# Turned one-hots from ScalarE out of the penalties, and seven tiles of a block weighed on VectorE, in a graph attention layer

## The chip, the core and the metric

The kernel runs on one core of one Trainium2 chip. The core has five engines with queues of their own: TensorE (PE; PEld for its weight loads), VectorE (DVE), ScalarE (ACT), GpSimd (POOL) and SyncE (SP). Each takes its instructions in the order in which they were written; between engines only semaphores keep order. The metric is device time in microseconds. A profile shows one execution.

## What is computed

Two graph layers with residual and layer norm on 20,000 nodes of 256 features, with 340,000 edges that are sorted by destination: a relational layer (two rounds of messages with a weight matrix for each of 8 edge types), then graph attention with four heads of 64 features. The change touches the attention alone:

```python
h = (x @ W).reshape(n, NHEAD, OUT_F)
hl = jnp.sum(a_l * h, axis=-1)
hr = jnp.sum(a_r * h, axis=-1)
e = jax.nn.leaky_relu(hl[row] + hr[col], negative_slope=ALPHA)
e_max = jax.ops.segment_max(e, row, num_segments=n)
...
ee = jnp.exp(e - e_max[row])
denom = jax.ops.segment_sum(ee, row, num_segments=n)
att = ee / denom[row]
msg = att[:, :, None] * h[col]
out_h = jax.ops.segment_sum(msg, row, num_segments=n)
...
x = _layernorm(x + _L1_gnn_ref(x, edge_index, L1_gnn_W, L1_gnn_a_l, L1_gnn_a_r), axis=-1)
```

For every node `row` the edges that start there compete: the greatest score is taken off, the exponentials are the weights, and the weighted rows `h[col]` are added up and divided by the sum of the weights.

## The kernel before

Nodes come in 157 blocks of 128, one node to a partition. The edges of a block are laid into 17 tiles of 128 edges (`T3 = 17`), one edge to a partition. Before the attention two rounds compute the relational layer, sort the edges by their other end and write a row of 270 float32 (1080 bytes) for each node into `table3s`: the 256 features of `h`, four `hr`, four `hl`, and `hr` once more in three bfloat16 parts.

The attention is `attention` with its function `step(i)`, called for i = 0 to 157 under an order written out by hand (`manual_schedule`): nothing is moved by a scheduler. Three blocks are in work in a step: a (block i), b (i - 1) and c (i - 2). Tiles carry the letters of the profile:

- `load(b)`, L1360: 17 gathers on POOL, each of which brings the `table3s` rows of a tile's 128 edges into `g`; L1358, a plain load on SP, brings the block's own rows as an eighteenth tile. Four buffers of `g` turn, so the gathers of block i + 2 wait until the last `sums` of block c = i - 2 is done.
- `load_ob`, L1344: five loads on SP, which spread the ids of each edge's own node over all partitions (`ob`, bfloat16, 128 x 17 x 128).
- `ends(a, 0..2)`, L1404 and L1406: TensorE turns the three parts of `hr` onto 12 rows, ScalarE copies them out (`hpt`). Parts are six, six and five tiles.
- `distances(a, 0..2)`, L1382: on ScalarE, `pen = (FAR * (ob - row))^2` with FAR = 2^50: 0 where the edge belongs to the node of this partition, at least 2^100 where not.
- `greatest(a, part, head)`, L1417 and L1420: TensorE spreads one head's `hr` of six tiles over all partitions (`pr`, two buffers), and VectorE takes `pr - pen` and its maximum along the row in one instruction. There are twelve in a step, 3 parts x 4 heads; the text calls them compares, one to twelve.
- `one_hots(a)`, L1388: on VectorE, `s[edge, node]` = 1 where the edge is the node's. It is the matrix by which `sums` adds up.
- `turned_hots(a)`, L1394: on VectorE, the same one-hots the other way round, `st[node, edge] = (ob == row)` in bfloat16, 128 x 2176 elements. In the next step `spread(b)`, L1440, multiplies by it to bring each node's terms to its edges.
- `own_terms(b)`, L1428 to L1431 and, through `split`, L1300 and L1303: small VectorE instructions on the maxima of block b. They open a step.
- `weights(b)`, L1445 to L1453: VectorE forms the scores, ScalarE the exponentials, once into PSUM (`pw`) and once into `g`. 
- `weigh_few(b, tiles)`, L1468: VectorE multiplies the 256 features of several tiles by their weights, in one instruction. `weigh(b, tiles)`, L1462: ScalarE does the same with four instructions of 128 x 64 for each tile, one a head.
- `sums(b, tiles)`, L1476: TensorE multiplies the one-hots by the weighted rows, in float32, and accumulates a block's 18 tiles in `po`.
- `finish`, `measure`, `write` (L1482 to L1513): quotient, residual, layer norm; `write` works on four blocks at a time, with a square root on ScalarE, so that every fourth step loads another function table and the step after it loads that of the exponential again.

The second half of `step` is a loop n = 1 to 9. Each turn has one `sums(b, [n])`, the weighing on ScalarE of a tile some turns ahead, and one or two further compares; `turned_hots` stands behind the compare of turn 5, `distances` of parts 1 and 2 in turns 1 and 3, `write` in turn 4. TensorE thus alternates between a compare's two matmuls, which wait for VectorE to have freed a `pr` buffer, and the two passes of a float32 `sums`, which wait for the weighing.

A last block with fewer than 8 tiles takes the branch `few`, once in the whole run.

Of the kernel before, what the change touches and what calls it, by code (L numbers as in the profile page):

```python
# [35 lines left out]
BF16 = mybir.dt.bfloat16  # L36
# [3 lines left out]
AF = mybir.ActivationFunctionType  # L40
ALU = mybir.AluOpType
# [6 lines left out]
P = 128  # L48
# [9 lines left out]
T3 = 17  # L58
# [16 lines left out]
def gnn_kernel(  # L75
# [17 lines left out]
    nc = tc.nc  # L93
# [83 lines left out]
    ones = const.tile([P, P], F32, name="ones")  # L177
# [8 lines left out]
    row_of = const.tile([P, 1], F32, name="row_of")  # L186
# [1120 lines left out]
    def attention(words):  # L1307
        with tc.tile_pool(name="ac", bufs=1) as cp, tc.tile_pool(name="ag", bufs=4) as gp, \
# [20 lines left out]
            parts = [(q, min(6, T3 - q)) for q in range(0, T3, 6)]  # L1329
# [35 lines left out]
            def others(k):  # L1365

                n = k["n"]
                k["ob"] = obs.pop(k["b"])
                k["pen"] = sp.tile([P, T3, P], BF16, name="pen")
                k["hpt"] = turns[k["b"] % 2]  # L1370

                k["top"] = sp.tile([P, H, 1 + len(parts)], F32, name="top")
                nc.scalar.copy(k["top"][:, :, 0], k["g"][:, n, D:SR])
                k["hl"] = sp.tile([P, 2, H], F32, name="hl")
                nc.scalar.copy(k["hl"][:, 0, :], k["g"][:, n, SR:SR + H])  # L1375

            def distances(k, i):

                q, m = parts[i]
                m = min(m, k["n"] - q)  # L1380
                if m > 0:
                    nc.scalar.activation(k["pen"][:, q:q + m], k["ob"][:, q:q + m], AF.Square, bias=away, scale=FAR)  # L1382

            def one_hots(k):

                s = k["s"] = sp.tile([P, T3, P], F32, name="s", bufs=3)
                n = k["n"]
                nc.vector.tensor_tensor(s[:, :n], pi.unsqueeze(1).to_broadcast([P, n, P]),  # L1388
                                        own3[:, k["b"], :n].unsqueeze(2).to_broadcast([P, n, P]), op=ALU.is_equal)

            def turned_hots(k):

                k["st"] = sp.tile([P, T3, P], BF16, name="st")
                nc.vector.tensor_scalar(k["st"][:, :k["n"]], k["ob"][:, :k["n"]], row_of, None, op0=ALU.is_equal)  # L1394

            def ends(k, i):

                q, m = parts[i]
                m = min(m, k["n"] - q)
                if m <= 0:  # L1400
                    return
                ph = p2.tile([P, 6, P], F32, name="pr")
                for t in range(q, q + m):
                    nc.tensor.matmul(ph[:3 * H, t - q, :], k["g"][:, t, SR + H:].bitcast(BF16), identb,  # L1404
                                     start=True, stop=True)
                nc.scalar.copy(k["hpt"][:3 * H, q:q + m, :], ph[:3 * H, :m, :])  # L1406
# [19 lines left out]
            def own_terms(k):  # L1426
                z = sp.tile([P, H], F32, name="z")
                nc.vector.tensor_reduce(z, k["top"][:, :, :1 + -(-k["n"] // 6)], op=ALU.max, axis=AX.X)  # L1428
                hl = k["hl"]
                nc.vector.tensor_add(z, z, hl[:, 0, :])  # L1430
                nc.vector.scalar_tensor_tensor(hl[:, 1, :], z, SLOPE, z, op0=ALU.mult, op1=ALU.max)  # L1431
                k["hlp"] = split(sp, hl.rearrange("p a h -> p (a h)"), [2 * H], "hlp")

            def spread(k):

                k["pe"] = p1.tile([P, 512], F32, name="pe")
                n = k["n"]
                pe = k["pe"][:, :(n + 1) * 6 * H].rearrange("p (t c) -> p t c", t=n + 1)
                for t in range(n + 1):
                    nc.tensor.matmul(pe[:, t], k["st"][:, t, :] if t < n else identb, k["hlp"], start=True, stop=True)  # L1440
# [14 lines left out]
            def weigh(k, ts):  # L1455

                for t in ts:
                    if t > k["n"]:
                        return
                    gh = k["g"][:, t, :D].rearrange("p (h f) -> p h f", h=H)  # L1460
                    for h in range(H):
                        nc.scalar.activation(gh[:, h, :], gh[:, h, :], AF.Copy, scale=k["g"][:, t, D + h:D + h + 1])  # L1462

            def weigh_few(k, ts):

                t, n = ts[0], len(ts)
                gh = k["g"][:, t:t + n, :D].rearrange("p t (h f) -> p t h f", h=H)
                nc.vector.tensor_mul(gh, gh, k["pw"][:, t:t + n, :].unsqueeze(3).to_broadcast([P, n, H, HF]))  # L1468

            def sums(k, ts):  # L1470
                n = k["n"]
                for t in ts:
                    if t == 0:
                        k["po"] = p2.tile([P, SR], F32, name="po")
                    if t <= n:
                        nc.tensor.matmul(k["po"], k["s"][:, t, :] if t < n else ident, k["g"][:, t, :SR],  # L1476
                                         start=(t == 0), stop=(t == n))
# [39 lines left out]
            def step(i):  # L1517

                a, b, c = (blocks.get(x) for x in (i, i - 1, i - 2))
                if b:
                    own_terms(b)
                if a:
                    others(a)
                    ends(a, 0)
                    distances(a, 0)
                if c:
                    sums(c, [11, 12])
                    weigh(c, [16])  # L1530
                if b:
                    spread(b)
                if a:
                    one_hots(a)
                if c:
                    sums(c, [13])
                if a:
                    ends(a, 1)
                if c:
                    weigh(c, [17])  # L1540
                    sums(c, [14])
                if a:
                    ends(a, 2)
                if c:
                    sums(c, [15, 16])
                if b:
                    load_x(b)
                if b and not a:

                    weights(b)  # L1550
                    for t in range(0, b["n"] + 1, 6):
                        weigh_few(b, list(range(t, min(t + 6, b["n"] + 1))))
                        sums(b, range(t, min(t + 6, b["n"] + 1)))
                    if c:
                        sums(c, [17])
                        finish(c)
                        measure(c)
                        write(c)
                    finish(b)
                    measure(b)  # L1560
                    write(b)
                    return
                if b:
                    weights(b)
                    weigh_few(b, [0, 1])
                    weigh_few(b, [2, 3, 4])
                if a:
                    greatest(a, 0, 0)
                if c:
                    sums(c, [17])  # L1570
                    if c["b"] + 4 < NB:
                        blocks[c["b"] + 4] = load(c["b"] + 4)
                load_ob(i + 2, 0)
                if a:
                    greatest(a, 0, 1)
                if b:
                    sums(b, [0])
                if a:
                    greatest(a, 0, 2)
                if c:  # L1580
                    finish(c)
                few = a and a["n"] < 8
                for n in range(1, 10):
                    if a and n in (1, 3):
                        distances(a, (n + 1) // 2)
                    if b:
                        sums(b, [n])
                        if few and n in (1, 4, 7):
                            weigh_few(b, [n + 5, n + 6])
                        if not few or n in (1, 4, 7):  # L1590
                            weigh(b, [n + 4])
                        if n == 9:
                            weigh(b, [14, 15])
                    if a:
                        greatest(a, (n + 2) // 4, (n + 2) % 4)
                        if n == 5:
                            turned_hots(a)
                    if n in (2, 4, 6, 8):
                        load_ob(i + 2, n // 2)
                    if c and n == 1:  # L1600
                        measure(c)
                    if c and n == 4:
                        write(c)
                if b:
                    sums(b, [10])
# [330 lines left out]
```

## Time and profile before

Five runs took 13794.76 to 13819.41 us, with a median of 13805.79 us.

| | |
|---|---|
| profiled execution, its own time | 13803.91 us |
| its span | 13801.8 us |
| mean granted TensorE clock | 0.852 |
| PE busy | 9911.7 us (72%) |
| PEld busy | 7524.2 us (55%) |
| DVE busy | 7552.4 us (55%) |
| ACT busy | 5946.9 us (43%) |
| POOL busy | 7624.3 us (55%) |

"Busy" sums the durations that an engine's instructions have in the record. A line of a group gives the line of code, the engine, the operation, what it writes from what, the count, then busy time and the mean of one in nanoseconds, then the engine's idle time just before them and what ended it. The largest groups of the attention, over the whole run:

```profile
L1360 POOL DMA_INDIRECT g<-table3s,words x2657 | 2540.3, 956 | 2826.5 <-PE po L1476 1999.6
L1420 DVE CUSTOM_DVE_ANT_0 dump<-pr,pen 128x768 bf16<-128x768 f32 x1876 | 1654.6, 910 | 1981.7 <-remote 1321.2
L1462 ACT ACTIVATE g<-g 128x64 f32<-128x64 f32 x8088 | 2065.1, 334 | 438.3 <-issue 437.9
L1476 PE MATMUL po<-g,s 128*128 128x260 f32 x5314 | 2025.1, 480 | 85.2 <-DVE g L1468 85.2
```

Instructions of an engine overlap at their ends, so the starts of two `weigh` instructions can lie closer together than the 334 ns that one lasts.

### The profile page before, as it was taken

The page shows a single profiled execution, that of the slowest core. Times are in us where ns is not written, and L with a number is a line of the kernel's source. Part 1 is how long each engine was busy: PE and PEld are TensorE (multiplying, and loading weights), DVE is VectorE, ACT ScalarE, POOL GpSimd, SP SyncE. Part 2 cuts the span into 40 slices and gives each one's busy share as a digit, 9 for nine tenths or more (in the row PEclk, how much of TensorE's full clock was granted, in tenths as well). Part 3 has the DMA queues.
Part 4 walks back from the last instruction along what each step waited for, and adds up shares of the span by engine and source line. Part 5 has one row for each costly group of instructions (what it writes and reads, how often), then busy time and mean ns, then how long its engine had stood idle before and what let it go on. Part 6 is the DMA issues. An engine that isn't in the chain of part 4 may idle for free. (4 is left out here: it accounts for less than half of the span.)

```text
span 13801.8 us, 220867 instructions
## 1 busy us (share of the span) xinstructions
PE 9911.7 (72%) x75815; PEld 7524.2 (55%) x75815; DVE 7552.4 (55%) x21335; ACT 5946.9 (43%) x18175; POOL 7624.3 (55%) x8041
## 2 busy tenths in 40 slices
PE   7888888888887888888888885555555555555555
PEld 6777766666666676767676663333333333333333
DVE  4455555556564555555555543555555555555556
ACT  2311114444443333333333333555555555555555
POOL 6666666666655565655565664444444444444443
PEclk8999999999998998999899997777777777777777
DMA  5655555445545555555555553333333333333332
GB/s 171 208 145 147 147 143 146 143 143 145 144 130 154 148 150 149 149 147 148 149 149 147 150 152 97 98 97 99 97 97 96 98 98 99 97 98 99 96 97 83
DMA packets 860287, 1777.62 MB, mean 129 GB/s; under 512 B 196892, under 2 KB 525834, under 8 KB 859130
## 3 DMA queue, kind: packets, MB, share of 16 engines
q0 software_dynamic: 461200, 1384.74, 36.2%
q1 hardware_dynamic: 390098, 371.45, 8.5%
q8 instruction: 597, 9.78, 0.3%
q10 hardware_dynamic: 7848, 7.20, 0.2%
q14 instruction: 544, 4.46, 0.1%
HBM read 1629.85 MB, written 132.98 MB: 128 GB/s over the span
## 5 line engine op out<-in xcount | busy, mean ns | idle before, releaser
L1360 POOL DMA_INDIRECT g<-table3s,words x2657 | 2540.3, 956 | 2826.5 <-PE po L1476 1999.6
L611 POOL DMA_INDIRECT g<-h2s,idx x2657 | 2518.0, 948 | 1738.7 <-PE a L732 1024.6
L732 PE MATMUL a<-s,g 128*128 128x152 bf16 (+9 forms) x34860 | 2989.6, 230 | 202.7 <-issue 160.4
L679 PE MATMUL pm<-wt,to 128*128 128x256 f32 x10624 | 2955.0, 401 | 26.6 <-issue 24.8
L611 POOL DMA_INDIRECT g<-xs,idx x2209 | 2104.1, 952 | 1307.0 <-PE a L732 589.3
L1420 DVE CUSTOM_DVE_ANT_0 dump<-pr,pen 128x768 bf16<-128x768 f32 x1876 | 1654.6, 910 | 1981.7 <-remote 1321.2
L1417 PE MATMUL pr<-hpt,pick 128*128 128x512 bf16 (+2 forms) x3752 | 1013.6, 357 | 2227.0 <-DVE top L1420 1116.3
L732 PEld LDWEIGHTS <-g 128*128 128x128 bf16 x32844 | 2245.2, 101 | 525.2 <-issue 273.8
L1462 ACT ACTIVATE g<-g 128x64 f32<-128x64 f32 x8088 | 2065.1, 334 | 438.3 <-issue 437.9
L1476 PE MATMUL po<-g,s 128*128 128x260 f32 x5314 | 2025.1, 480 | 85.2 <-DVE g L1468 85.2
L679 PEld LDWEIGHTS pm<-wt,to 128*128 128x128 f32 x10624 | 1846.6, 194 | 238.1 <-issue 63.3
L1417 PEld LDWEIGHTS <-pick 128*128 128x128 bf16 x3752 | 389.6, 104 | 2811.2 <-issue 2693.7
L1147 DVE CUSTOM_DVE_ANT_0 dump<-pr,b 128x157 f16<-128x157 f32 x2657 | 714.2, 320 | 1683.9 <-PE pr L1127 645.8
L656 ACT COPY to<-a 128x512 f32<-128x512 f32 x996 | 553.7, 584 | 2252.7 <-PE a L732 1739.9
L1476 PEld LDWEIGHTS po<-g,s 128*128 128x128 f32 x5314 | 1011.8, 230 | 508.3 <-issue 225.5
L971 DVE TENSOR_TENSOR b<-pi,kb 128x471 f16<-128x471 f32 (+1 forms) x1798 | 1109.3, 634 | 277.0 <-PE a L732 123.6
L1137 ACT ACTIVATE two<-b,words 128x157 f16<-128x157 f16 x2657 | 1124.6, 423 | 299.7 <-DVE b L971 121.0
L1138 ACT ACTIVATE two<-b,words 128x157 f16<-128x157 f16 x2657 | 1102.8, 415 | 0.0
L1406 ACT CAST hpt<-pr 12x768 bf16<-12x768 f32 (+1 forms) x469 | 350.1, 747 | 1609.9 <-PE pr L1404 1609.4
L634 DVE TENSOR_TENSOR s<-pi,code 128x1216 bf16<-128x1216 f32 x610 | 859.9, 1410 | 0.0
L1165 PE MATMUL pl<-two,a 128*128 128x314 f16 x2657 | 536.9, 312 | 204.5 <-DVE a L1153 137.8
L675 PE MATMUL pm<-wt,ot 128*128 128x256 f32 x1328 | 539.0, 548 | 120.3 <-issue 79.1
(290 smaller groups left out, 10715.3 us busy)
## 6 DMA issues: line engine op xcount, KB each, us to landing
ob<-ownd SPq DMA_DIRECT2D x625, 128.0 KB
g<-h2s,idx POOLq DMA_INDIRECT x2657
g<-table3s,words POOLq DMA_INDIRECT x2657
g<-xs,idx POOLq DMA_INDIRECT x2209
h2s<-h SPq DMA_DIRECT2D x166, 192.0 KB
own<-h2s SPq DMA_DIRECT2D x166, 192.0 KB
xs<-xs SPq DMA_DIRECT2D x156, 192.0 KB
own<-xs SPq DMA_DIRECT2D x136, 192.0 KB
```

The lines of the kernel that those rows point to most:

```text
L611: nc.gpsimd.indirect_dma_start(out=g, out_offset=None, in_=of, in_offset=bass.IndirectOffsetOnAxis(ap=idx[u // CS][:, u % CS:u % CS + 1], ...
L634: nc.vector.tensor_tensor(s, pi[:, :w].unsqueeze(1).to_broadcast([P, e - f, w]), codes(c, e - f).unsqueeze(2).to_broadcast([P, e - f, w]), ...
L679: nc.tensor.matmul(p, to[:, i % 2, i // 2, :P], wt[:, i % 2, i // 2, :], start=False, stop=(i == 2 * R - 1))
L732: nc.tensor.matmul(a[h, q][:, b:e, :].rearrange("p n r -> p (n r)"), g[:, v * D + h * P:v * D + (h + 1) * P], s, start=((h, q) not in begu ...
L971: nc.vector.tensor_tensor(b[:, :n], pi[:, :NB].unsqueeze(1).to_broadcast([P, n, NB]), self.k["kb"][:, c:c + G * (n - 1) + 1:G].unsqueeze(2 ...
L1137: nc.scalar.activation(two[:, 0, :], made[m][:, x, :], AF.Copy, scale=k["hi"][:, c:c + 1])
L1138: nc.scalar.activation(two[:, 1, :], made[m][:, x, :], AF.Copy, scale=k["lo"][:, c:c + 1])
L1360: nc.gpsimd.indirect_dma_start(out=g[:, t, :], out_offset=None, in_=table3s, in_offset=bass.IndirectOffsetOnAxis(ap=to3[:, b, t:t + 1], ax ...
L1417: nc.tensor.matmul(pr[:, t:t + n, :], pick[:, h, :], k["hpt"][:, q + t:q + t + n, :], start=True, stop=True)
L1420: nc.vector.tensor_tensor_reduce(out=dump[:, :m, :].rearrange("p t e -> p (t e)"), in0=pr[:, :m, :].rearrange("p t e -> p (t e)"), in1=k[" ...
L1462: nc.scalar.activation(gh[:, h, :], gh[:, h, :], AF.Copy, scale=k["g"][:, t, D + h:D + h + 1])
L1476: nc.tensor.matmul(k["po"], k["s"][:, t, :] if t < n else ident, k["g"][:, t, :SR], start=(t == 0), stop=(t == n))
```

## The change

`turned_hots` moves from VectorE to ScalarE and is cut into the three parts that `distances` has. It no longer reads `ob` but the penalties: `max(0, 1 - pen)` is 1 where the penalty is 0 and 0 elsewhere. Its parts stand in turns 2, 4 and 6 of the loop instead of as a whole in turn 5. `weigh_few` takes tiles 0 to 6 in two instructions of three and four tiles, instead of tiles 0 to 4 in two of two and three; `weigh` on ScalarE starts with tile 7 in turn 3, instead of with tile 5 in turn 1. The branch for a short last block is fitted to that.

```diff
-            def turned_hots(k):
-
-                k["st"] = sp.tile([P, T3, P], BF16, name="st")
-                nc.vector.tensor_scalar(k["st"][:, :k["n"]], k["ob"][:, :k["n"]], row_of, None, op0=ALU.is_equal)
+            def turned_hots(k, i):
+
+                q, m = parts[i]
+                m = min(m, k["n"] - q)
+                if i == 0:
+                    k["st"] = sp.tile([P, T3, P], BF16, name="st")
+                if m > 0:
+                    nc.scalar.activation(k["st"][:, q:q + m], k["pen"][:, q:q + m], AF.Relu, bias=ones[:, 0:1],
+                                         scale=-1.0)
...
                     weights(b)
-                    weigh_few(b, [0, 1])
-                    weigh_few(b, [2, 3, 4])
+                    weigh_few(b, [0, 1, 2])
+                    weigh_few(b, [3, 4, 5, 6])
...
                         sums(b, [n])
-                        if few and n in (1, 4, 7):
+                        if few and n in (4, 7):
                             weigh_few(b, [n + 5, n + 6])
-                        if not few or n in (1, 4, 7):
+                        if few and n == 1:
+                            weigh(b, [7])
+                        if n > 2 and not few or n in (4, 7):
                             weigh(b, [n + 4])
                         if n == 9:
                             weigh(b, [14, 15])
                     if a:
                         greatest(a, (n + 2) // 4, (n + 2) % 4)
-                        if n == 5:
-                            turned_hots(a)
+                        if n in (2, 4, 6):
+                            turned_hots(a, n // 2 - 1)
```

## The prediction

> **What bounds the kernel now.** I read the 40 slices first, then the waits of the attention stage, then busy time by stretches of one step, then single instructions.
>
> ```profile
> PE   7888888888887888888888885555555555555555
> DVE  4455555556564555555555543555555555555556
> ACT  2311114444443333333333333555555555555555
> POOL 6666666666655565655565664444444444444443
> PEclk8999999999998998999899997777777777777777
> ```
>
> The change sits in the attention stage, the last 16 slices. There no engine is above 6 tenths, so nothing is bound by busy time; waits decide. The 157 steps begin at 8522 us (first reduction of `own_terms`); 145 regular ones, read from the trace, last 34.1 us in the mean. Over 9000 to 13700 us the waits are:
>
> ```profile
> POOL g L1360 <- PE po L1476: 1764.0, 136, 14.4
> ...
> DVE dump L1420 <- remote: 1170.0, 250, 9.0
> PE pr L1417 <- DVE top L1420: 989.0, 456, 8.9
> ...
> DVE dump L1420 <- issue: 485.2, 100, 7.5
> ACT g L1462 <- issue: 398.8, 573, 1.8
> DVE g L1468 <- ACT pe L1452: 237.0, 138, 3.7
> ```
>
> Each step, VectorE stands (1170.0 + 485.2) / 138 = 12.0 us in front of a compare (L1420, twelve a step) though the matmul that feeds it is recorded as done. One step from 10997.70 us in three stretches:
>
> ```profile
> core 0: us, PE busy (x) PEld busy (x) DVE busy (x) ACT busy (x) POOL busy (x), PEclk, DMA share, GB/s
> ...
> 10997.70:11012.50 14.80, 11.08 (x72) 6.97 (x72) 11.85 (x30) 13.57 (x41) 6.10 (x7) 0.94 0.38 106
> 11012.50:11028.50 16.00, 4.52 (x17) 2.28 (x16) 4.20 (x9) 6.01 (x24) 10.01 (x11) 0.73 0.38 102
> 11028.50:11032.70 4.20, 3.12 (x9) 1.52 (x9) 3.26 (x9) 0.00 (x0) 0.00 (x0) 0.50 0.00 0
> ```
>
> First a full stretch; then 16 us in which only the gathers run at their pace and VectorE finishes a compare every 6 to 7 us; when the last gather has landed, the rest is cleared. I call the middle one the slow stretch. The trace does not show its cause; it shows its edges. It opens 9 to 11 us after the first gather and closes with the gathers: on average they start at 7.2, the last is issued at 27.3 and lands at 30.5 us of the step. What remains sets the end. With three compares left after the landing a step ends 3.12 us after it (103 steps), with four 4.37 us (5 steps of the same kinds), with two 2.19 us (2 steps). So **step = gather start + gathers and landing (23.3 us) + 2.2, 3.1 or 4.4 us by what is left**. Work before the slow stretch counts only through that number.
>
> Steps come in four kinds, by their place in a group of four: W writes four blocks (Sqrt table), X loads the Exp table again, then Y and Z. Means, from the step's start:
>
> | | W | X | Y | Z |
> |---|---|---|---|---|
> | first `weigh_few` | 6.61 | 8.24 | 6.28 | 6.67 |
> | eighth compare | 16.5 | 27.3 | 18.1 | 20.9 (ninth: 28.6) |
> | ninth compare | 23.3 | 31.5 | 25.0 | 28.6 |
> | step | 33.7 | 35.5 | 33.3 | 34.0 |
>
> **The change, part by part.** Durations of the same window:
>
> ```profile
> L1382 ACT ACTIVATE pen<-ob,away 128x768 bf16<-128x768 bf16 x276 | 255.1, 924 | 0.0
> ...
> L1468 DVE TENSOR_TENSOR g<-g,pe 128x768 f32<-128x768 f32 x137 | 129.7, 947 | 0.0
> L1394 DVE TENSOR_SCALAR st<-ob,row_of 128x2176 bf16<-128x2176 bf16 x138 | 111.6, 809 | 0.0
> L1382 ACT ACTIVATE pen<-ob,away 128x640 bf16<-128x640 bf16 x137 | 111.2, 812 | 0.0
> L1468 DVE TENSOR_TENSOR g<-g,pe 128x512 f32<-128x512 f32 x138 | 95.0, 688 | 237.0 <-ACT pe L1452 237.0
> ```
>
> 1. *Seven tiles on VectorE.* 947 - 688 = 259 ns for a third tile, so two more cost 0.52 us, ahead of all twelve compares. This is not covered in the first stretch: compares one to six go back to back. No gather waits for it: POOL waits for `sums(c, [17])`, which stands before the first matmul that needs `weigh_few`. The first `sums(b, [0])` comes 0.26 us later, still ahead of the third compare, which TensorE waits for next anyway.
>
> 2. *`turned_hots` off VectorE.* Minus 0.81 us and minus its two semaphore instructions, between compares eight and nine. Compare nine waits for its matmul then, so VectorE gains next to nothing at that place: I take 0, bounds 0 and 0.8 us a step. But it frees POOL:
>
> ```profile
> 11050.41 0.95 POOL L1360 DMA_INDIRECT g<-table3s,words  x1 [0.30 <-issue]
> 11051.67 1.30 POOL L1360 DMA_INDIRECT g<-table3s,words  x1 [0.30 <-issue]
> 11053.27 0.94 POOL L1360 DMA_INDIRECT g<-table3s,words  x1 [0.30 <-DMA g<-table3s,words]
> ```
>
> `turned_hots` began at 11051.36; the one gather beside it took 1.30 for 0.95 us. Sixteen issues span 20.05 us in X, 20.08 in W, 20.33 in Y, 20.20 in Z: 0.28 + 0.15 us gone from Y and Z, 39 steps each, **17 us** in all.
>
> 3. *The turned one-hots on ScalarE.* The trace has no such Relu with a per-partition bias; by the nearest rows it lies between 747 ns (the mean of the casts, L1406) and 924 ns. I take L1382's, same shape and bias operand: starts follow each other by 0.83, 0.83 and 0.72 us, so +2.38 us. Eight weighings less, 0.24 us apart: -1.91 us. Net **+0.47 us** of ScalarE a step, bounds 0 and +0.5. Cover: it is done at 23.9 us in the mean (30.9 in W) and its next work, the cast of the following step, comes at 34.5. Without that cover 157 x 0.47 = 74 us. `spread` needs `st` after 35 us. Compares five and nine need `distances`: the first is not moved, the second is earlier by 1.91 - 0.83 = 1.1 us; weighing of tile 7, the first that TensorE awaits from ScalarE, likewise. The compiled order has 39 table loads at either place before and after; the same DMAs are issued by SP and POOL in the same order; the broadcast loads of `ob` lose only their wait for VectorE, of three steps back.
>
> The Trainium skill speaks against this part: "ScalarE: Activation LUTs", Rules for kernel authors, sends relu and its like to VectorE, up to three times faster in bf16. The rows agree on the price (0.81 against 2.38 us), and by that rule alone the move would lose 1.6 us a step; with ScalarE idle at the end of a step it loses nothing. The other way, "GPSIMD Engine Reference", Key points, says GpSimd shares its SBUF interfaces with VectorE instructions in a two-port mode; the 1.30 us gather agrees.
>
> 4. *Fewer instructions ahead of the slow stretch.* Eight fewer ScalarE instructions are out when it opens. W is the trial of that: ScalarE waits there, some 12.5 fewer are out, and the ninth compare comes 16.1 us after the first gather, against 18.1 in Y and 21.3 in Z: 3.6 us earlier, 0.29 us per instruction, so 2.3 us for eight. X is the trial of part 1: its compares start 1.4 us later against the gathers, and the eighth comes 7.8 us later; 5.5 us per us, so 0.52 us makes 2.9. Net: late compares +0.6 us. Bounds: -2 (relief worth nearly twice that) and +2.9 (no relief).
>
> Sum at +0.6 us: no kind changes its number of compares left, but some 4 of the 39 Z steps (ninth compare already past 29.7), 4 x 1.25 = 5 us. So -17 + 5 = -12 us. The profiled execution took 13803.91 us (span 13801.8), 2 us under the median of 13805.79; on the median that is **13794, say 13795 us**.
>
> **The rivals.**
> *Relief wins.* At -2 us the tenth compare, 6.9 us behind the ninth, starts before the landing in W (21.3 + 6.9) and in half of Y: 39 x 0.93 + 19 x 0.93 = 54 us, with 17 from the gathers: 13735. For it: ScalarE meets its own slow starts after 42 to 44 instructions counted from the first gather, in W as in X, Y and Z, though W gets there 5 us later; so counts matter. Against it: three long instructions may weigh more than eight short ones.
>
> *Shift wins (slower).* Place: the compares before the slow stretch. Price 1.25 us for each step that keeps one more. At +2.9 us all Z (28.6 + 2.9 = 31.5) and half of X (27.3 + 2.9 = 30.2, against a landing at 30.7; some 0.9 us each) slip: 49 + 18 - 17 = +50 us, 13856. It decides from +1.1 us on, where half of Z (median 29.2) is past 30.3. For it: X, which pays for a late start today. Against it: W.
>
> *ScalarE becomes the bound.* Only if its last instruction passes 34 us; in W it ends at 30.9, plus 0.5. Then up to 74 us more, 13880.
>
> **How the numbers follow.** The cancelling case 40%, own range 13770 to 13825; relief 25%; shift 32%; ScalarE 3%. A measurement here tells 0.2%, 28 us, from no change: 13778 and 13833 are the bounds. Faster: 0.3 x 40 + 25 = 37%. Same: 0.6 x 40 = 24%. Slower: 0.1 x 40 + 32 + 3 = 39%. The range reaches over both rivals' middles, less their far tails: 13685 to 13900.
>
> **What would show it.** `turned_hots` gone from VectorE, no gather above 1.0 us, Y and Z gathers in 20.05 us; `weigh_few` at 947 and some 1206 ns; three ScalarE rows like L1382's; gather start still at 7.2 us. The count of compares after the landing tells which case it is: waits of L1420 at 12.0 us a step if I am right, less if relief wins. I am wrong if the slow stretch's edges move by more than 0.3 us, or the step changes with that count unchanged.

## The result, and the profile after

The changed kernel takes 13820.34 us (median of 24 runs), the kernel before 13809.77 us in the 44 runs that now stand beside it. The ratio is 1.0007, 95% interval 1.0002 to 1.0013: about 10 us slower, inside the range and inside the 0.2% that I called no change, but on the other side of the forecast of -12 us. (Ratios and intervals here are formed from all runs of a pair, not from the two medians, and can differ from these in the fourth digit.) The profiled execution took 13821.47 us (span 13819.8).

The 40 slices of the changed kernel hardly differ from those before:

```profile
PE   7888888888887888888888884555555555555555
...
DVE  4455556556654555555555543555555555555556
ACT  2311114444443333333333333555555555555556
POOL 6666666666655555555555564444444444444443
PEclk9899999999998999999999987777777777777778
```

Nor does busy time tell much. The groups of the attention over the whole run (lines of the new code are five higher, L1420 is now L1425):

```profile
L1360 POOL DMA_INDIRECT g<-table3s,words x2657 | 2540.4, 956 | 2845.6 <-PE po L1481 2018.4
...
L1425 DVE CUSTOM_DVE_ANT_0 dump<-pr,pen 128x768 bf16<-128x768 f32 x1876 | 1659.8, 910 | 2076.6 <-remote 1211.0
...
L1481 PE MATMUL po<-g,s 128*128 128x260 f32 x5314 | 1993.7, 473 | 125.7 <-ACT pen L1382 123.2
...
L1467 ACT ACTIVATE g<-g 128x64 f32<-128x64 f32 x6848 | 1746.4, 333 | 225.7 <-issue 224.0
```

The parts cost what was said. These are groups between 9000 and 13700 us by form: the new one-hots on ScalarE (L1398) and the two instructions of `weigh_few` (L1473):

```profile
L1398 ACT ACTIVATE st<-pen,ones 128x768 bf16<-128x768 bf16 x274 | 251.6, 918 | 0.0
...
L1473 DVE TENSOR_TENSOR g<-g,pe 128x1024 f32<-128x1024 f32 x137 | 166.2, 1214 | 0.0
...
L1473 DVE TENSOR_TENSOR g<-g,pe 128x768 f32<-128x768 f32 x137 | 130.7, 954 | 188.0 <-ACT pe L1457 188.0
L1398 ACT ACTIVATE st<-pen,ones 128x640 bf16<-128x640 bf16 x137 | 111.2, 812 | 0.0
```

And the waits of the same window:

```profile
POOL g L1360 <- PE po L1481: 1785.4, 136, 15.2
...
DVE dump L1425 <- remote: 1072.1, 249, 9.0
PE pr L1422 <- DVE top L1425: 1011.7, 374, 8.9
...
DVE dump L1425 <- issue: 617.6, 117, 7.2
ACT g L1467 <- issue: 202.7, 298, 1.8
DVE g L1473 <- ACT pe L1457: 188.0, 137, 3.8
```

ScalarE waits less (202.7 for 398.8 us), but VectorE stands as long in front of its compares: (1072.1 + 617.6) us over the 137 steps of the window are 12.3 us a step, for 12.0. The slow stretch is as it was. What changed is which compares lie before it.

One step of the changed kernel, of kind Z, from 9570.64 us: VectorE's instructions in order of time (start, duration, and in brackets the idle time before and what ended it):

```profile
9581.86 0.42 DVE L1492 TENSOR_TENSOR o<-o,xb 128x256 f32<-128x256 f32 x1
...
9587.59 0.96 DVE L1425 CUSTOM_DVE_ANT_0 dump<-pr,pen 128x768 bf16<-128x768 f32 x1 [2.10 <-remote]
...
9593.94 0.96 DVE L1425 CUSTOM_DVE_ANT_0 dump<-pr,pen 128x768 bf16<-128x768 f32 x1 [5.38 <-remote]
...
9601.03 0.82 DVE L1425 CUSTOM_DVE_ANT_0 dump<-pr,pen 128x640 bf16<-128x640 f32 x1 [6.13 <-issue]
...
9601.78 0.82 DVE L1425 CUSTOM_DVE_ANT_0 dump<-pr,pen 128x640 bf16<-128x640 f32 x1
...
9604.16 0.82 DVE L1425 CUSTOM_DVE_ANT_0 dump<-pr,pen 128x640 bf16<-128x640 f32 x1 [0.68 <-PE pr L1422]
```

and POOL's in the same step, with the idle time before each:

```profile
9576.96 0.94 POOL L1360 DMA_INDIRECT g<-table3s,words  x1 [13.26 <-PE po L1481]
...
9580.73 0.95 POOL L1360 DMA_INDIRECT g<-table3s,words  x1 [0.30 <-issue]
9581.98 1.12 POOL L1360 DMA_INDIRECT g<-table3s,words  x1 [0.30 <-issue]
9583.41 0.95 POOL L1360 DMA_INDIRECT g<-table3s,words  x1 [0.30 <-issue]
```

Two things are to be seen. The stretch closes with the compare at 9601.03, 24.07 us after the first gather (9576.96), with the ninth compare: four are left. And the gather at 9581.98 takes 1.12 for 0.95 us, beside the residual add (L1492): `turned_hots` is gone from VectorE, but another instruction lengthens a gather. The place of the add counts. Here it begins shortly before the gather; in the kernel before it falls on a gather's end or just ahead of one:

```profile
11009.58 0.94 POOL L1360 DMA_INDIRECT g<-table3s,words  x1 [0.30 <-issue]
11010.35 0.42 DVE L1487 TENSOR_TENSOR o<-o,xb 128x256 f32<-128x256 f32 x1
```

Of the gathers that such an add overlaps, 111 of 154 last over 1.0 us in the changed kernel, all of them with the add over their first 0.2 to 0.3 us; in the kernel before none of 176 does.

Over all steps the trace gives a better split than mine. In the kernel before, the compare that closes the slow stretch starts 24.02 us after the first gather in the median, 90% of them between 23.95 and 24.11, whether the gathers land early or late (22.5 to 23.9 us after the first; correlation with the landing 0.14). Nor does it follow the issue of the last gather (20.0 to 20.6 us; correlation -0.06). So **step = gather start + close + rest**, where the rest is 1.61, 2.5, 4.0 or 5.6 us with two, three, four or five compares left (the closing one counted in). Means over the 145 regular steps of one profiled execution each, in us; counts are steps with 2, 3, 4, 5 left:

| kernel | gather start | close | rest | step | 2 / 3 / 4 / 5 left |
|---|---|---|---|---|---|
| before | 7.21 | 24.02 | 2.89 | 34.11 | 2 / 103 / 40 / 0 |
| changed | 6.87 | 23.86 | 3.52 | 34.24 | 5 / 59 / 63 / 18 |
| changed, again | 6.84 | 23.80 | 3.52 | 34.15 | 4 / 63 / 58 / 20 |
| seven tiles alone | 6.73 | 23.89 | 3.54 | 34.16 | 28 / 19 / 79 / 19 |
| one-hots alone | 7.23 | 24.02 | 2.90 | 34.14 | 2 / 102 / 41 / 0 |
| shift alone | 6.81 | 23.94 | 3.44 | 34.19 | 0 / 65 / 70 / 10 |
| eight weighings less | 7.17 | 24.00 | 2.82 | 33.99 | 37 / 55 / 53 / 0 |
| gathers first | 6.81 | 23.93 | 3.30 | 34.05 | 2 / 64 / 79 / 0 |
| clock kept up | 6.88 | 23.99 | 3.27 | 34.14 | 2 / 98 / 45 / 0 |
| weighing moved | 7.40 | 23.92 | 2.37 | 33.69 | 63 / 52 / 27 / 0, and 3 with 1 |

The two rows of the changed kernel differ by 0.09 us a step, so a step is compared between executions to about 0.1 us, which is 16 us over the run and more than the 10 us by which the kernels differ; the counts are steadier. For the changed kernel the split reads: rest +0.63 us a step, 99 us over 157 steps; gather start -0.34, -53 us; close -0.16, -25 us; together +21 us in this pair of executions, +10 in the medians. A loss of 99 us is there, and nearly four fifths of it come back in two terms that my sum did not have.

### The profile page after: what moved, and what is told of

Its sections match the earlier page's. It is cut to its first block, busy times and chain, and to the rows that moved or that the text cites. A ratio compares the mean times of both kernels' runs of the same rounds, so it can differ in the third digit from the quotient of the medians.

```text
span 13819.8 us, 219738 instructions
## 1 busy us (share of the span) xinstructions
PE 9870.9 (71%) x75815; PEld 7501.2 (54%) x75815; DVE 7530.9 (54%) x21177; ACT 5969.9 (43%) x17404; POOL 7624.9 (55%) x8041
## 5 line engine op out<-in xcount | busy, mean ns | idle before, releaser
L1425 DVE CUSTOM_DVE_ANT_0 dump<-pr,pen 128x768 bf16<-128x768 f32 x1876 | 1659.8, 910 | 2076.6 <-remote 1211.0
L1481 PE MATMUL po<-g,s 128*128 128x260 f32 x5314 | 1993.7, 473 | 125.7 <-ACT pen L1382 123.2
L1467 ACT ACTIVATE g<-g 128x64 f32<-128x64 f32 x6848 | 1746.4, 333 | 225.7 <-issue 224.0
```

Of the source, the lines that this page charges most:

```text
L1425: nc.vector.tensor_tensor_reduce(out=dump[:, :m, :].rearrange("p t e -> p (t e)"), in0=pr[:, :m, :].rearrange("p t e -> p (t e)"), in1=k[" ...
```

## The experiments

All edits are made to the kernel before, unless the diff shows otherwise.

**Part 1 alone.** Seven tiles on VectorE, one-hots still there.

```diff
-                    weigh_few(b, [0, 1])
-                    weigh_few(b, [2, 3, 4])
+                    weigh_few(b, [0, 1, 2])
+                    weigh_few(b, [3, 4, 5, 6])
...
-                        if not few or n in (1, 4, 7):
+                        if n > 2 and not few or n in (4, 7):
                             weigh(b, [n + 4])
```

> Part 1 alone: VectorE weighs seven tiles, the turned one-hots stay on VectorE. Theory A (what VectorE does before the slow stretch counts, through the number of compares left after the last gather has landed, and a late step hands part of it back because TensorE's clock is higher when the next step opens): the ninth compare comes some 2.5 to 4.5 us later after the first gather than before (before: 16.1, 18.1 and 21.3 us in W, Y, Z), steps with four or more compares left rise from 41 to about 80 of 145, the first gather is issued 0.2 to 0.4 us earlier in the step, and the time is 10 to 35 us above before. Theory B (the three long ScalarE instructions are what delays the compares, and the eight short ones that fall away help, as the prediction had it): compares as in the kernel before or earlier, the time 0 to 30 us below before.

13818.44 against 13812.29 us, 1.0001 (0.9992 to 1.0010). The ninth compare comes 23.2 us after the first gather in Y (18.2 before) and 23.8 in Z (21.3), the eighth in X 23.0 (20.2); in W the ninth comes earlier, 12.8 for 16.1. So the shift is all of the loss in X, Y and Z, and the relief by eight ScalarE instructions is real in W alone, where 28 of 37 steps have two left.

**Parts 2 and 3 alone.** The one-hots on ScalarE, five tiles as before.

```diff
-            def turned_hots(k):
+            def turned_hots(k, i):
...
-                nc.vector.tensor_scalar(k["st"][:, :k["n"]], k["ob"][:, :k["n"]], row_of, None, op0=ALU.is_equal)
...
+                    nc.scalar.activation(k["st"][:, q:q + m], k["pen"][:, q:q + m], AF.Relu, bias=ones[:, 0:1],
+                                         scale=-1.0)
```

> Part 2 and 3 alone: the turned one-hots on ScalarE, VectorE weighs five tiles as before. Theory A: compares and first gather stay where they were (ninth compare within 1 us, 41 steps with four left, give or take 10); the 17 us that VectorE's turned one-hots added to the gathers go, so the time is 0 to 20 us below before. Theory B: ninth compare later by 2 us or more, as in the changed kernel, and the time 10 to 50 us above before.

13812.43 against 13812.29 us, 1.0001 (0.9992 to 1.0010). Here the gain at the gathers does come: what the gathers of the attention lose against their pitch of 1.253 us falls from 18.4 us over the run to 0.3. It brings nothing. One Y step of this kernel, VectorE first:

```profile
11330.42 0.82 DVE L1425 CUSTOM_DVE_ANT_0 dump<-pr,pen 128x640 bf16<-128x640 f32 x1 [5.47 <-remote]
...
11337.34 0.82 DVE L1425 CUSTOM_DVE_ANT_0 dump<-pr,pen 128x640 bf16<-128x640 f32 x1 [6.09 <-remote]
```

and its first and last gather on POOL:

```profile
11313.34 0.95 POOL L1360 DMA_INDIRECT g<-table3s,words  x1 [14.01 <-PE po L1481]
...
11333.40 0.95 POOL L1360 DMA_INDIRECT g<-table3s,words  x1 [0.30 <-issue]
```

The last gather is issued 20.06 us after the first, without delay, and this step's gathers land early, at 29.52 us of the step; VectorE still waits until 11337.34, 24.00 us after the first gather. The close does not follow the gathers' end. The 2.38 us on ScalarE cost nothing either: the cover held.

**The shift alone.** One more VectorE instruction behind `weigh_few`, which writes a tile that nobody reads.

```diff
                     weigh_few(b, [2, 3, 4])
+                    nc.vector.tensor_tensor(pad, pi[:, :64].unsqueeze(1).to_broadcast([P, 7, 64]), pad, op=ALU.is_equal)
```

> The kernel before with one added VectorE instruction of about 0.55 us (448 elements, result unused) behind weigh_few; ScalarE's work is untouched. Theory A: the same as with seven tiles: ninth compare 2.5 to 4.5 us later, about 80 steps with four or more left, first gather 0.2 to 0.4 us earlier in the step, time 10 to 50 us above before. Theory B: VectorE's 0.55 us is absorbed by the slow stretch: time within 10 us of before, first gather unmoved.

13825.02 us, 1.0008 (0.9999 to 1.0017). About half a microsecond of nothing does what the whole change does: Y's ninth compare at 22.6, Z's at 23.3, X's eighth at 22.2 us after the first gather; rest +0.55 us a step; and the gather start comes down by 0.39 us, though nothing was done to it.

**The relief alone.** Tiles 5 and 6 are not weighed, so that eight ScalarE instructions are gone without a shift.

```diff
-                        if not few or n in (1, 4, 7):
+                        if n > 2 and not few or few and n in (1, 4, 7):
                             weigh(b, [n + 4])
```

> The kernel before, but tiles 5 and 6 of a block are not weighed (that product is left out): eight short ScalarE instructions less ahead of the slow stretch, VectorE untouched. The prediction's part 4 (0.29 us per ScalarE instruction less): ninth compare 2.3 us earlier, the tenth before the landing in W and some of Y, time 20 to 50 us below before. Theory A: the number of ScalarE instructions does not matter: ninth compare within 0.7 us, time within 12 us of before.

13791.14 us, 0.9984 (0.9975 to 0.9993). In W the ninth compare comes 4.9 us earlier (11.1 for 16.1), 36 of 37 steps have two left. In Y it comes at 19.6 for 18.2, in Z at 22.5 for 21.3: later, not earlier, and 16 Z steps have four left for 4. X's eighth moves from 20.2 to 20.9 us. The relief of 0.29 us per instruction does not exist in X, Y and Z.

**Four runs on another chip.** The next four ran on a chip on which the kernel before took 10381.31 us, at a mean clock of 0.975; it was timed there, and only the edited kernels left profiles. They are an earlier trial of "weighing moved" and of "clock kept up" (diffs below), five buffers of `g` instead of four, and a memset on POOL ahead of each gather:

```diff
-        with tc.tile_pool(name="ac", bufs=1) as cp, tc.tile_pool(name="ag", bufs=4) as gp, \
+        with tc.tile_pool(name="ac", bufs=1) as cp, tc.tile_pool(name="ag", bufs=5) as gp, \
...
+                        nc.gpsimd.memset(idle, 0.0)
                     nc.gpsimd.indirect_dma_start(
```

> The kernel before with VectorE's weighing moved out of the first stretch: weigh_few takes tiles 0 and 1 ahead of the compares (0.69 us instead of 1.55) and tiles 11 to 13 in turn 7, inside the slow stretch; ScalarE weighs tiles 2 to 10 in the turns, as many instructions as before. Theory A (work before the slow stretch is paid through the compares left after it, work inside it is free): compares 0.8 us earlier against the first gather, the ninth 2 to 5 us earlier, fewer steps with four left than 41 and more with two left than 2; the next steps open later by up to 0.3 us because the clock is lower; time 15 to 80 us below before. Theory B (the place of VectorE's weighing does not matter, or TensorE now waits for ScalarE's tiles 2 and 3): compares unmoved or later, time within 10 us of before or above it.

> The kernel before with ten added bf16 matmuls of 128 x 240 (their product is read by nobody) on TensorE behind the sums of turn 9, where it waits for the tenth compare; not in the steps of kind X. Theory A (the next step opens sooner after a late step because TensorE's granted clock is higher): clock in the first 3.4 us of the steps that follow up from 0.60 to 0.70 or more, their first gather 0.2 to 0.5 us earlier in the step, time 10 to 60 us below before. Theory B (the clock is only a companion of late steps, the opening has another cause, or the added matmuls hold up the twelfth compare): first gather unmoved, time equal or above before.

> Five buffers of g instead of four, each block's gathers issued one block further ahead, so that POOL no longer waits for the last sums of block c. Theory A (the slow stretch is tied to gathers in flight: every step carries one, whenever they start): the gathers run on without a pause or nearly so, the slow handoffs spread over the whole step, and the time moves little, within 300 us of before either way. Theory B (a step is long because its gathers start late): the step falls from 34.1 us to 25 to 29 us, the time by 800 us or more.

> The kernel before with a small POOL memset (128 x 256, unused) ahead of every gather of the attention from the fifth block on, so that gathers follow each other by 1.5 to 1.8 us instead of 1.25. Theory A (the slow stretch closes with the gathers): the tenth compare moves from 23.9 us after the first gather to 28 to 33 us, the step grows by about as much, the time by 600 us or more. Theory B (the slow stretch comes from the rate of the gathers, or lasts a fixed time): the tenth compare stays at 24 us or comes sooner, the step grows by less than 2 us or shrinks.

Ratios 1.0007 (0.9998 to 1.0016), 1.0012 (1.0003 to 1.0021), 1.0002 (0.9992 to 1.0011) and 1.0495 (1.0476 to 1.0514). They tell nothing of the theories in their expectations, because there is no slow stretch on that chip. The waits of the first of them, between 7300 and 10200 us:

```profile
PEld L1417 <- issue: 699.9, 1313, 1.5
POOL g L1360 <- issue: 669.0, 2196, 0.3
PE pr L1417 <- DVE top L1420: 347.9, 471, 1.2
...
DVE dump L1420 <- PE pr L1417: 135.6, 86, 3.3
```

No compare waits on "remote" or "issue", POOL never waits for `sums`, and a step lasts 21.6 us, which is 17 gathers 1.27 us apart in the mean. Only the run that spreads the gathers (1.47 us apart, steps of 25.0 us) changes the time by more than 0.12%. So the slow stretch is not in the program's order: the same instructions run without it. What makes it on the one chip is open. The changed kernel was not run on this chip.

**The changed kernel again**, on a chip of the first kind.

> The changed kernel itself again, as a yardstick beside the next three. The runs so far came on two chips: on one the kernel before takes 13810 us and shows the slow stretch, on the other 10381 us with attention steps of 21.3 us, in which POOL issues gathers without a pause (17 x 1.254 us). On the first kind of chip: 5 to 15 us above before, with four or more compares left in about 80 of 145 steps and the first gather 0.2 to 0.4 us earlier in the step. On the second kind (theory A: POOL sets the step there, so only what lengthens a gather counts; the turned one-hots on VectorE lengthen one gather a step by 0.35 us, 41 us in all): 15 to 45 us below before. Theory B (VectorE's or ScalarE's order counts on the second kind too): within 10 us of before or above.

13809.00 against 13796.66 us, 1.0008 (0.9999 to 1.0017), with the same split (see the table).

**Does the clock give the refund?** With more left, a step ends busier, and the next opens sooner. In the trace of the changed kernel TensorE is busy for 0.65, 0.93 and 1.00 of a step's last 3.4 us with three, four and five left. The first 3.4 us of a step have a mean granted clock of 0.65 after three left, 0.83 after four and 0.91 after five, and the first gather then starts at 7.20, 6.66 and 6.44 us (correlation of start and clock -0.92). Two openings of that kernel, each with the stretch ahead of it; the first follows a step with five left, the other one with three:

```profile
core 0: us, PE busy (x) PEld busy (x) DVE busy (x) ACT busy (x) POOL busy (x), PEclk, DMA share, GB/s
9672.00:9675.44 3.44, 3.44 (x11) 1.56 (x9) 2.06 (x7) 0.00 (x0) 0.00 (x0) 0.50 0.00 0
9675.44:9678.84 3.40, 3.40 (x38) 2.52 (x37) 3.16 (x9) 2.56 (x6) 0.00 (x0) 0.84 0.01 2
10558.02:10561.42 3.40, 3.00 (x9) 1.37 (x8) 2.42 (x7) 0.00 (x0) 0.00 (x0) 0.50 0.01 3
10561.42:10564.82 3.40, 3.40 (x31) 2.57 (x30) 3.16 (x9) 2.56 (x6) 0.00 (x0) 0.62 0.00 0
```

At 0.84 TensorE does 38 matmuls in the first 3.4 us, at 0.62 it does 31; the gathers, which wait for `sums(c, [17])`, start at 6.58 and at 7.32 us. To take the compares out of it, ten matmuls that add to nobody's result go behind the `sums` of turn 9, in all kinds but X (`po` is made wider to take them):

```diff
+            def warm(k):
+                for _ in range(10):
+                    nc.tensor.matmul(k["po"][:, 272:], identb, pick.rearrange("p h q -> p (h q)")[:, :240], start=False, stop=False)
...
                         sums(b, [n])
+                        if n == 9 and a and i % 4 != 2:
+                            warm(b)
```

> Ten added bf16 matmuls of 128 x 240, product unused, behind the sums of turn 9, not in steps of kind X (as in the run with the label e6_warm). On the first kind of chip, theory A (the opening of a step is quicker when TensorE's granted clock is higher): clock in the first 3.4 us up from 0.60 to 0.70 or more in the steps that follow W, Y and Z, first gather 0.2 to 0.5 us earlier there, time 10 to 60 us below before. Theory B (the clock only accompanies late steps): first gather unmoved, time at or above before. On the second kind of chip: 0 to 20 us above before, since TensorE's added work brings nothing where POOL sets the step.

13783.80 us, 0.9991 (0.9982 to 1.0000). After steps with three left the clock of the next opening rises from 0.60 to 0.74 and the first gather comes at 6.93 us instead of 7.34. One opening and the stretch ahead of it, in this kernel (columns as above):

```profile
9681.34:9684.74 3.40, 3.40 (x22) 2.21 (x20) 2.41 (x6) 0.00 (x0) 0.00 (x0) 0.72 0.00 0
9684.74:9688.14 3.40, 2.85 (x32) 2.03 (x32) 3.16 (x9) 2.74 (x7) 0.00 (x0) 1.00 0.00 0
```

The granted clock is 1.00 there, TensorE even stands idle for half a microsecond, and the gathers start at 6.33 us. In the kernel before, three openings of kind W also had a clock of 0.95 to 1.00; they start their gathers at 6.32 to 6.33 us, without added matmuls. So a higher clock at the opening brings the earlier start, with no VectorE instruction moved in the program. The mean clock does not tell all of it: at 0.56 to 0.66 the openings of W and Z after three left start at 6.98 us with the added matmuls (12 openings) and at 7.35 us in the kernel before (51). Most of the refund is paid back: the ten matmuls hold up the last compares, the rest with three left grows from 2.49 to 2.80 us.

**Weighing moved into the idle stretch.** If only what lies ahead of the slow stretch counts, the opposite of part 1 must gain: VectorE weighs two tiles ahead of the compares and three in turn 7, where it waits; ScalarE weighs tiles 2 to 10 in the turns, as many as before.

```diff
-                    weigh_few(b, [0, 1])
-                    weigh_few(b, [2, 3, 4])
+                    weigh_few(b, [0, 1] if a and a["n"] >= 8 else [0, 1, 2, 3, 4])
...
-                        if not few or n in (1, 4, 7):
+                        if few and n in (1, 4, 7):
                             weigh(b, [n + 4])
+                        if not few:
+                            weigh(b, [n + 1])
+                        if not few and n == 7:
+                            weigh_few(b, [11, 12, 13])
```

> VectorE's weighing moved behind the first compares: tiles 0 and 1 ahead of them, tiles 11 to 13 in turn 7; ScalarE weighs tiles 2 to 10 (as in the run with the label e5_late). On the first kind of chip, theory A (work before the slow stretch is paid through the compares left, work inside it is free): ninth compare 2 to 5 us earlier after the first gather, fewer than 41 steps with four left, more than 2 with two left, next steps opening up to 0.3 us later, time 15 to 80 us below before. Theory B: compares unmoved, time within 10 us of before or above. On the second kind: within 15 us of before.

13713.13 against 13796.66 us, 0.9940 (0.9927 to 0.9954): 83 us faster than the kernel before, and so faster than both. Its waits between 9000 and 13600 us:

```profile
POOL g L1360 <- PE po L1476: 1691.7, 135, 14.5
...
DVE dump L1420 <- remote: 1036.2, 219, 8.3
PE pr L1417 <- DVE top L1420: 807.8, 234, 7.2
...
DVE dump L1420 <- issue: 402.3, 104, 6.8
```

The compares wait (1036.2 + 402.3) us over 136.5 steps, 10.5 us a step for 12.0. The ninth compare comes 14.6 us after the first gather in Y and 16.1 in Z, 63 steps have two left. The gather start rises by 0.19 us: the refund works backwards, and takes 30 us of the gain.

**Gathers ahead of the first compare.** `sums(c, [17])` and the 17 gathers are issued before the first compare's matmuls.

```diff
-                if a:
-                    greatest(a, 0, 0)
                 if c:
...
+                if a:
+                    greatest(a, 0, 0)
                 load_ob(i + 2, 0)
```

> The kernel before with the last sums of block c (and the gathers that wait for it) ahead of the first compare's two matmuls instead of behind them; nothing else. On the first kind of chip, theory A (step = gather start + 23.9 us + what is left): first gather 0.3 to 0.6 us earlier, the slow stretch closes that much earlier, but one more compare may be left; time 20 to 90 us below before. Theory B (the step's end does not follow the gather start): time within 12 us of before. On the second kind, where POOL never waits for the last sums: within 10 us of before.

13789.94 us, 0.9993 (0.9984 to 1.0002). The gathers start 0.39 us earlier, at 6.81, but against them every compare stands later (Y's ninth at 22.8 for 18.2), 79 steps have four left for 40: rest +0.41 us. An earlier gather start and a later compare are the same thing to the slow stretch.

## Why the prediction was right or wrong

*What bounds the kernel: right, with one edge wrong.* The three stretches and the price by compares left hold in every kernel of the table, all on this kind of chip, but for "clock kept up", whose added matmuls raise the price of three and four left by 0.3 and 0.4 us. That the stretch "closes with the gathers" is wrong: it closes some 24.0 us after the first one is issued, landing or not. In the kernel before both read alike, since the landing lies at 23.3 us in the mean.

*Part 1, seven tiles: right.* +0.53 us, ahead of all compares (954 and 1214 ns for 688 and 947).

*Part 2, one-hots off VectorE: "-17 us" failed.* Zero at its own place was right. At the gathers the gain was there in "one-hots alone" and worth nothing, because of the edge above: the time between landing and close was idle. In the changed kernel it was not even there: the shift brought the residual add onto the first part of a gather, in 109 steps, 0.18 us each, 19.9 us in all for the 18.4 that went. The Trainium skill, "GPSIMD Engine Reference", Key points, names both kinds of partner, the two-port mode and two SBUF inputs; I used the first and overlooked that L1487, an add of two SBUF tiles, is of the second. The traces agree with it in part: 1.30 and 1.12 for 0.95 us, but only where the two meet at certain places (74 of the 155 gathers beside `turned_hots` in the kernel before, and none of the 176 beside the add). So the kernel before showed no price for the add.

*Part 3, ScalarE: right.* 918 and 812 ns; ScalarE's last work of a step ends at 22.8 us in the mean, 31.0 in W. By the rule of the Trainium skill that sends relu to VectorE ("ScalarE: Activation LUTs", Rules for kernel authors) the move would have cost 1.6 us a step; "one-hots alone" at 1.0001 (0.9992 to 1.0010) measures no loss, to within some 14 us.

*Part 4, the relief of 2.3 us: the step that failed and decided.* I took it from W, against Y and Z, and carried it to all kinds. "Eight weighings less" shows 4.9 us in W and none in Y and Z. Without it the shift of 0.53 us acts alone, at the bound that I had kept for that: "no relief", 2.9 us. X's eighth compare came 2.6 us later, Z's ninth 1.9, Y's 4.8. So the rival "shift wins" is what happened, and went further: 24 of 36 Z steps and 21 of 36 Y steps have four left, half of X five. Slips cost 99 us, where my sum had 5 and the rival's 67. (X's eighth compare stands at 27.6 us in the kernel before, not at 27.3 as in my table; no conclusion turns on it.)

*What no case had: the refund.* "Gather start still at 7.2 us" was wrong; it fell to 6.87. A longer rest keeps TensorE busier at the end of a step, the next opening gets a higher clock, and the first gather starts 2.7 to 2.9 us sooner per unit of clock. That is -53 us. The Trainium skill, "TensorE: Matmul & The Clock Gate", Part 1: The HAM clock gate, says that the default is a throttled clock, which some 3.4 us of activity release; the rows agree (0.50 at the end of a step, 0.62 to 1.00 in the next opening). The other -25 us come from 35 steps of 145 (3 before) that close at 23.3 instead of 24.0 us; what decides that is open. So the time fell near the forecast through a loss and two refunds, not through the two small terms that I had set against each other. Of the signs that I named, the wait in front of the compares was no use: it reads 12.3 us a step for 12.0, as if I were right. The count of compares left tells the case.

Left open: why VectorE learns of a finished matmul 5 to 6 us late while gathers run, on one kind of chip and not on the other; why fewer ScalarE instructions help in W alone; what fixes the close at 24.0 us (the gathers were spread on the other kind of chip alone).

## What to carry to other kernels

Where a step has a stretch of fixed length in which an engine waits, count what is left behind it, not busy time: work moved from ahead of that stretch into it gained 0.6%, while half a microsecond added ahead of it moved the late compares by 2.0 to 4.4 us and the rest of a step by 0.55. This was seen on the chips with the stall alone. A relief or a price that is measured in one kind of step is tried in the others before it enters a sum. And before a kernel is tuned around a stall, look whether the stall is there on another chip of the same model.

## What the hardware showed that I had not expected

- The kernel before, the same program, takes 13.80 ms on some chips and 10.38 ms on another. On the slower ones compares stand 12 us a step in front of matmuls that are recorded as done; in the edits of it that were profiled on the faster one not at all, with the same pitch of gathers (1.25 us in the median on both).
- The close of that stretch keeps to 24.0 us after the first gather within 0.1 us in most steps of ten executions, with a second place at 23.3 us.
- A gather of 0.95 us can be lengthened by a VectorE instruction beside it: by 0.27 us in the mean of 74 gathers beside a bfloat16 comparison of 128 x 2176, by 0.18 us in 111 beside a float32 add of two 128 x 256 tiles. About as many beside the comparison, and 43 beside the add, were not lengthened; it depends on where in the gather the two meet.
- Ten small matmuls at the end of a step raise the granted clock of the next step's first 3.4 us from 0.60 to 0.74 in the mean.
